# A macaron stack on one core: attention's order of work, routing from logits, and when the last mixture's rows are scattered

## The chip, the core and the metric

The kernel runs on one core of a Trainium2 chip. The metric is the device time of one execution in microseconds (us). The core has TensorE (matrix products and transposes), VectorE, ScalarE and GpSimd (called POOL in the profile), and SyncE (SP), which here issues the plain DMAs; the indirect DMAs, which scatter rows to addresses held in a tile, are issued by POOL. An engine runs its instructions in the order in which the program issued them.

## The reference

Four layers work on x of 4 batches x 512 tokens x 128 channels. Every layer is a macaron: half an FFN, an attention, half an FFN again, each on a layer norm of x.

```python
x = x + 0.5 * ffn(layernorm(x)); x = x + attn(layernorm(x)); x = x + 0.5 * ffn(layernorm(x))
```

- Layer 0: the FFN is a mixture of 8 experts, one choice per token, capacity 320; the attention is causal with 16 heads of 8 and a bias table added to the scores.
- Layer 1: the FFN is a mixture in which every expert is computed for every token; the attention is causal, with no table, and its scores are a product of two factor products.
- Layer 2: the FFN is a two-choice mixture without capacity; in the attention's place stands a gated recurrence.
- Layer 3: the attention is plain (no causal mask); the FFN is a mixture of 8 experts with two choices and capacity 512. Its routing is what most of the diff is about:

```python
scores = softmax(xt @ wg); gates_k, idx_k = top_k(scores, 2)
gates_k = gates_k / sum(gates_k)
m = one_hot(idx_k) as (2*T, E)                 # all first choices, then all second ones
loc = cumsum(m) - 1                            # a token's place in its expert's queue
valid = loc < cap                              # the others are dropped
y = sum_k gates_k * valid * expert_out[idx_k, loc]
```

In layer 0 the choice is the argmax, its weight the largest softmax value, and the place a cumulative sum of the one-hot rows.

## The kernel before

**Mixtures.** `Mixture` holds one expert FFN with scattered tokens: f00 and f01 (layer 0, before and after its attention), f30 and f31 (layer 3). `tokens(bs, ...)` norms the batches `bs` (statistics on VectorE, reciprocal root on POOL by L157/L158, application on VectorE, ScalarE or POOL), transposes, computes the logits on TensorE (L322), chooses (`softmax`, `route`, `without` on VectorE), computes each token's place with two matmuls per choice into `rank` (a triangular matrix of ones on the masks, and a full one on the running sums `pre`), turns it into a row number `to` (L385), copies the weights (L392) and issues one indirect DMA per 128 tokens and choice on POOL (L395, "scatter" below). Places run on from batch to batch through `self.cum`, so the batches' tokens steps follow one another there. `experts` fetches rows from the scattered buffer by SP (`d_f`), transposes them (`dT_f`, L442), and runs two matrix products; it can start only when every scatter of the mixture has landed. `tokens` is a generator: each `yield` ends a step, and the caller decides what is issued between two steps.

**Attention.** `attention` serves layers 0, 1 and 3. A unit is one batch and four heads: 16 units. In the causal layers (the path with `added`, the table or a mask) a unit has four steps, one for each 128 queries, of 128, 256, 384 or 512 keys. The scores of unit u+1 are computed while unit u is worked off: TensorE makes four score banks (L587), VectorE adds the mask and finds the row's extreme in one instruction (L604, L608); POOL subtracts it for two of the four heads (L605), ScalarE takes the exponential of the other two (L617). Four steps later TensorE transposes them (L628), ScalarE takes the exponential of POOL's two (L637) or copies (L639), and TensorE multiplies by the values (L650). In between, each step has two slots for other work: the next batch's `begin` (norm, transposes by `turned`, projections) and, when that is not due, the `after` work of a finished batch: in layer 0 that is f01's `tokens`, with `fine=True`, which cuts it into smaller steps. Layer 1 has layer 3's weights beside it.

All four computing engines' order in `attention` is that of the program text (`manual_schedule`). Between layers 1 and 3 a chain (`behind`) runs FFN, FFN, recurrence, FFN and f30's tokens for batches 0 and 1 together, and 2 and 3 behind them; there POOL's order alone is that of the text and the others' is the scheduler's. In the chain, f30's tokens of the first pair have `later=4`, four empty rounds ahead of the scatters.

**PSUM.** All matmul results share one pool of eight banks (`bank`), given out in rotation.

**Start.** f00's routing runs beside the build of layer 0's bias table: its rows are written to DRAM and read back reversed (`rev`), and TensorE turns them (`turned`, L948).

Of the kernel before, what the change touches and what calls it, by code (L numbers as in the profile page):

```python
# [17 lines left out]
P = 128  # L18
# [23 lines left out]
def kernel(ctx: ExitStack, tc: tile.TileContext, a: dict, out: bass.AP):  # L42
# [25 lines left out]
    for b in range(NB):  # L68
# [13 lines left out]
    before = const([P, P], "before")  # L82
    nc.gpsimd.affine_select(
        out=before, in_=ones, pattern=[[1, P]], compare_op=ALU.is_gt, fill=0.0, base=0, channel_multiplier=-1
    )
    mhalf = const([P, 2 * NT], "mhalf")
# [102 lines left out]
    def turned(n, tag):  # L189

        nT = work.tile([P, S], FP, name=f"nT_{tag}", tag="nT", bufs=4)
        copy(nT, transposed(n, tag))
        yield
        return nT
# [10 lines left out]
    def route(pool, src, g, tag, mask=None):  # L205

        mx = pool.tile([P, g], FP, name=f"mx_{tag}", tag=f"mx_{tag}")
        nc.vector.tensor_reduce(mx, src, AX.X, ALU.max)
# [14 lines left out]

    def softmax(pool, lg, g, tag):

        mx = pool.tile([P, g], FP, name=f"smx_{tag}", tag=f"smx_{tag}")
        nc.vector.tensor_reduce(mx, lg, AX.X, ALU.max)
        pr = pool.tile([P, g, E], FP, name=f"pr_{tag}", tag=f"pr_{tag}")
        nc.vector.tensor_tensor(pr, lg, bc(mx, [P, g, E]), ALU.subtract)
        nc.scalar.activation(pr, pr, AF.Exp)  # L230
        yield
        sm = pool.tile([P, g], FP, name=f"sm_{tag}", tag=f"sm_{tag}")
        nc.vector.tensor_reduce(sm, pr, AX.X, ALU.add)
        nc.vector.reciprocal(sm, sm)
        nc.vector.tensor_tensor(pr, pr, bc(sm, [P, g, E]), ALU.mult)
        return pr
# [4 lines left out]
    class Mixture:  # L241
# [18 lines left out]

        def zeroed(self, pool, tag, bufs=None):

            self.z = pool.tile([P, S], FP, name=f"zeros_{self.tag}", tag=tag, bufs=bufs)
            nc.gpsimd.memset(self.z, 0.0)
# [18 lines left out]
        def tokens(self, bs, wT, on="vector", pool=None, fine=False, later=0):  # L283
# [8 lines left out]
            for n, b in zip(ns, bs):  # L292
# [8 lines left out]

            spare = pool.tile([P, k, G], FP, name=f"spare_{tag}", tag=f"spare{k}{G}")
            nc.gpsimd.tensor_scalar(
                spare, bc_mid(tok_id[:, i0 : i0 + G], [P, k, G]), float(self.rows), None, ALU.add
            )
# [28 lines left out]
            pr = yield from softmax(pool, plg[:, : G * E].rearrange("p (g e) -> p g e", e=E), G, f"r{G}")  # L334
# [15 lines left out]
            if fine:  # L350
                yield
# [1210 lines left out]
```

## Time and profile before

| what | us |
|---|---|
| median of 11 runs | 1558.69 (1554.69 to 1563.63) |
| the profiled execution, its time | 1559.83 |
| its span | 1558.1 |
| TensorE busy in it | 1283.9 (82%) |
| f00: routing; experts | 0 to 60; 61 to 112 |
| layer 0 attention, f01's tokens | 113 to 386 |
| f01: experts; layer 1 FFN | 386 to 540 |
| layer 1 attention | 540 to 790 |
| chain of layers 1 and 2, f30's tokens | 780 to 1047 |
| f30: experts | 1054 to 1121 |
| layer 3 attention, f31's tokens | 1121 to 1465 |
| f31: experts, combine | 1471 to 1558 |

The bounds of the stages are read from the trace and overlap a little. Times are of one profiled execution. A line of a timeline has start, duration, engine, source line, operation, written tile <- read tiles, shape and count, and in brackets how long the engine had stood idle and what released it. A line of waits has who waited, for whom, the sum in us, how often, and the longest. The granted clock is the share of TensorE's full clock that the chip's throttle let through.

### The profile page before, as it was taken

The numbers are of one execution on the slowest core, as the hardware profiler recorded it, in microseconds if no ns is written. First come the engines' busy times: TensorE is split into PE (matmuls) and PEld (weight loads), VectorE is DVE, ScalarE is ACT, GpSimd is POOL, SyncE is SP. The second block draws the span as 40 slices with busy tenths as digits, with TensorE's granted clock in tenths as the row PEclk, the third lists the DMA queues.
The fourth block names the chain that finished last, engine by engine and source line by source line (L and its number), as shares of the span: only waits on it lengthen the run. The fifth ranks groups of instructions, "written<-read, shape, count | busy, mean of one in ns | idle before, by whom it ended". The sixth has DMA issues, their size and how long they took to land. (4 is left out here: it accounts for less than half of the span.)

```text
span 1558.1 us, 28883 instructions
## 1 busy us (share of the span) xinstructions
PE 1283.9 (82%) x10651; PEld 826.0 (53%) x10651; DVE 866.1 (56%) x2955; ACT 712.6 (46%) x1487; POOL 655.7 (42%) x791
## 2 busy tenths in 40 slices
PE   3787998995969688989989887819789999998394
PEld 3464676774755455757656666706533334333273
DVE  5325666773335366666555556615367787773342
ACT  1234876772443156768743322203336655564041
POOL 3455766772420177677610111263631224212253
PEclk9997999996989888999999878858979999999597
DMA  7420230002415375442022000014204000000233
GB/s 227 129 63 7 77 145 31 9 3 62 145 50 110 96 219 147 135 138 69 2 57 54 1 0 1 10 60 103 61 21 171 15 5 12 13 3 15 75 81 103
DMA packets 100660, 106.21 MB, mean 68 GB/s; under 512 B 9084, under 2 KB 73832, under 8 KB 100520
## 3 DMA queue, kind: packets, MB, share of 16 engines
q1 hardware_dynamic: 93864, 91.16, 20.7%
q0 software_dynamic: 6656, 13.22, 2.6%
q8 instruction: 84, 1.38, 0.4%
q14 instruction: 56, 0.46, 0.1%
HBM read 62.49 MB, written 41.85 MB: 67 GB/s over the span
## 5 line engine op out<-in xcount | busy, mean ns | idle before, releaser
L605 POOL TENSOR_SCALAR sc_a<-sc_a,top_a 128x128 f32<-128x128 f32 (+3 forms) x256 | 275.4, 1091 | 115.4 <-DVE top_a L604 77.2
L587 PE MATMUL s_a<-k_a,q_a 32*128 32x512 f32 (+3 forms) x1536 | 266.5, 550 | 17.2 <-DMA k_a<-fac_a 13.8
L692 ACT ACTIVATE w_a<-t_a 128x512 f32<-128x512 f32 x256 | 140.3, 595 | 119.6 <-PE t_a L587 94.8
L628 PE MATMUL t_a<-ident,sc_a 128*128 128x128 f32 x1280 | 173.5, 283 | 5.8 <-DVE top_a L608 5.3
L489 POOL DMA_INDIRECT res_f<-y_f,back_f x112 | 109.6, 979 | 143.6 <-ACT y_f L488 102.7
L587 PE MATMUL t_a<-ql_a,k_a 32*128 32x512 f32 x512 | 168.8, 645 | 0.4 <-DVE low_a__12755 L672 0.2
L628 PEld LDWEIGHTS t_a<-ident,sc_a 128*128 128x128 f32 x1280 | 146.3, 145 | 36.9 <-issue 14.1
L617 ACT ACTIVATE sc_a<-sc_a,top_a 128x128 f32<-128x128 f32 (+3 forms) x256 | 135.0, 577 | 23.2 <-DVE top_a L608 22.9
L587 PEld LDWEIGHTS s_a<-k_a,q_a 32*128 32x128 f32 x1536 | 93.1, 189 | 88.0 <-issue 43.2
L637 ACT ACTIVATE w_a<-t_a 128x256 f32<-128x256 f32 (+2 forms) x192 | 94.3, 526 | 64.4 <-PE t_a L628 64.0
L395 POOL DMA_INDIRECT disp_f<-n_f,to_f x96 | 94.3, 982 | 66.8 <-issue 58.8
L501 PE MATMUL o_f<-w_l,h_f 128*128 128x128 f32 (+1 forms) x896 | 113.0, 279 | 3.8 <-DVE o_f L483 3.3
L501 PEld LDWEIGHTS o_f<-w_l,h_f 128*128 128x128 f32 (+1 forms) x896 | 103.0, 184 | 14.7 <-DVE o_f L483 6.0
L466 PE MATMUL h_f<-dT_f,w_l 128*128 128x320 f32 (+1 forms) x256 | 108.1, 560 | 2.8 <-ACT dT_f L444 2.8
L157 POOL TENSOR_SCALAR rs_f<-mv_f 128x4 f32<-128x4 f32 (+1 forms) x23 | 5.7, 247 | 230.3 <-DVE mv_f L154 229.6
L650 PE MATMUL acc_a<-w_a,vpad 128*32 128x128 f32 x2560 | 98.5, 280 | 0.6 <-DVE top_a L604 0.6
L672 DVE TENSOR_REDUCE low_a__12755<-s_a 128x1 f32<-128x512 f32 x128 | 82.1, 684 | 26.3 <-PE t_a L587 18.5
L639 ACT COPY w_a<-t_a 128x256 f32<-128x256 f32 (+2 forms) x192 | 93.6, 528 | 6.0 <-PE t_a L628 5.8
L608 DVE CUSTOM_DVE_ANT_0 sc_a<-s_a,future 128x128 f32<-128x128 f32 (+3 forms) x128 | 62.3, 486 | 56.4 <-PE s_a L587 43.4
L608 DVE CUSTOM_DVE_ANT_0 sc_a<-s_a,table 128x128 f32<-128x128 f32 (+3 forms) x128 | 62.4, 487 | 54.7 <-PE s_a L587 54.2
L672 DVE TENSOR_REDUCE low_a__12753<-s_a 128x1 f32<-128x512 f32 x128 | 81.2, 682 | 20.1 <-PE t_a L587 15.1
L488 ACT ACTIVATE y_f<-o_f,d_f 128x128 f32<-128x128 f32 (+1 forms) x112 | 38.8, 394 | 105.9 <-DVE o_f L483 105.9
(343 smaller groups left out, 2289.1 us busy)
## 6 DMA issues: line engine op xcount, KB each, us to landing
fac_a<-fac_a_sb SPq DMA_DIRECT2D x36, 256.0 KB
disp_f<-zeros_f SPq DMA_DIRECT2D x4, 2080.0 KB
d_f<-disp_f SPq DMA_DIRECT2D x32, 260.0 KB
w_l<-in_L_ffn_w_dram SPq DMA_DIRECT2D x16, 512.0 KB
cb_f<-rows_f SPq DMA_DIRECT2D x16, 512.0 KB
q_a<-fac_a SPq DMA_DIRECT2D x32, 256.0 KB
k_a<-fac_a SPq DMA_DIRECT2D x32, 256.0 KB
r_f<-res_f SPq DMA_DIRECT2D x24, 256.0 KB
```

The lines of the kernel that those rows point to most:

```text
L395: nc.gpsimd.indirect_dma_start(out=self.to[c][i0 + t][:, :], out_offset=bass.IndirectOffsetOnAxis(ap=to[:, c, t : t + 1], axis=0), in_=ns[ ...
L466: nc.tensor.matmul(ps[u][:, :cap], w1[:, e, (c + u) * P : (c + u + 1) * P], dT, start=True, stop=True)
L489: nc.gpsimd.indirect_dma_start(out=self.back[e * per + s][:, :], out_offset=bass.IndirectOffsetOnAxis(ap=back[:m, s : s + 1], axis=0), in_ ...
L501: nc.tensor.matmul(po[:m, s, :], h[:, c, s * P : s * P + m], w2[:, e, c, :], start=(c == 0), stop=(c == NC - 1),)
L587: nc.tensor.matmul(ps[:, n0:n1], q[r : r + SLOT, i * P : (i + 1) * P], k[r : r + SLOT, n0:n1], start=True, stop=True)
L605: nc.gpsimd.tensor_scalar(sc, sc, top, None, ALU.subtract)
L608: nc.vector.tensor_tensor_reduce(sc, banks[r][:, :n], more, -1.0, HUGE, ALU.add, ALU.min, top)
L617: nc.scalar.activation(sc, sc, AF.Exp, bias=top, scale=-1.0)
L628: nc.tensor.transpose(ps[:, x * n + j * P : x * n + (j + 1) * P], st["sc", u, i, r0 + x][:, j * P : (j + 1) * P], ident,)
L650: nc.tensor.matmul(st["acc", u][r * SLOT : (r + 1) * SLOT, i * P : (i + 1) * P], vpads[b % 2][:, j, g * 4 + r, :], st["w", u, i, r][:, j * ...
L672: nc.vector.tensor_reduce(st["low", u][:, i, c : c + 1], ps, AX.X, ALU.max, negate=True)
L692: nc.scalar.activation(w, ps, AF.Exp)
```

## The change

- **Routing** (all four mixtures): the first choice is taken from the logits, not from softmax values; the exponentials of logits less their maximum serve the second choice and the weights (1 over the sum, or over 1 plus the second's exponential). The masks lie as choice, expert, tile; one scan with a mask of zeros at each expert's first tile (`goes_on`) makes the running sums, and the matmuls take all choices at once, with `not_before` (ones less one) in place of `before`, and a third one for the carried `cum` from the second call on. Spare row numbers and the ends of the experts' queues are made once per mixture on VectorE. Weights are computed behind the rank matmuls, and the row number needs no `keep`.
- **f30's tokens of the first pair:** `later=4` goes; `apart=True` yields after every scatter, and two steps are taken per round of the chain. On POOL the order was: norms of batch 2, norms of batch 3, copies, 16 scatters, 8 and 8. Now: copies and 10 scatters, norms of batch 2, 6 scatters, norms of batch 3, 8 and 8.
- **`turned`:** one more step ahead of the transposes and one behind.
- **Causal attention:** the first of the two slots of a step moves ahead of the next unit's scores, and POOL's subtractions move into `exponentials()`, which is called a step later.

```diff
@@ -79,10 +79,17 @@
-    before = const([P, P], "before")
+    not_before = const([P, P], "not_before")
     nc.gpsimd.affine_select(
-        out=before, in_=ones, pattern=[[1, P]], compare_op=ALU.is_gt, fill=0.0, base=0, channel_multiplier=-1
+        out=not_before, in_=ones, pattern=[[1, P]], compare_op=ALU.is_gt, fill=0.0, base=0, channel_multiplier=-1
     )
+    nc.vector.tensor_scalar(not_before, not_before, -1.0, None, ALU.add)
+    goes_on = {}
+    for g in (NT, 2 * NT):
+        goes_on[g] = const([P, 2 * E * g], f"goes_on{g}")
+        nc.vector.memset(goes_on[g], 1.0)
+        nc.vector.memset(goes_on[g].rearrange("p (e t) -> p e t", t=g)[:, :, 0], 0.0)
...
@@ -188,8 +195,10 @@
     def turned(n, tag):
+        yield
         nT = work.tile([P, S], FP, name=f"nT_{tag}", tag="nT", bufs=4)
         copy(nT, transposed(n, tag))
+        yield
         yield
         return nT
@@ -202,10 +211,11 @@
         return ap.unsqueeze(1).to_broadcast(shape)
-    def route(pool, src, g, tag, mask=None):
-        mx = pool.tile([P, g], FP, name=f"mx_{tag}", tag=f"mx_{tag}")
-        nc.vector.tensor_reduce(mx, src, AX.X, ALU.max)
+    def route(pool, src, g, tag, mask=None, mx=None):
+        if mx is None:
+            mx = pool.tile([P, g], FP, name=f"mx_{tag}", tag=f"mx_{tag}")
+            nc.vector.tensor_reduce(mx, src, AX.X, ALU.max)
         eq = pool.tile([P, g, E], FP, name=f"eq_{tag}", tag=f"eq_{tag}")
...
@@ -220,20 +230,6 @@
         rest = pool.tile([P, g, E], FP, name=f"rest_{tag}", tag=f"rest_{tag}")
         nc.vector.scalar_tensor_tensor(rest, mask, low, src, ALU.mult, ALU.add)
         return rest
-    def softmax(pool, lg, g, tag):
-        mx = pool.tile([P, g], FP, name=f"smx_{tag}", tag=f"smx_{tag}")
-        nc.vector.tensor_reduce(mx, lg, AX.X, ALU.max)
...
-        return pr
     routing = ctx.enter_context(tc.tile_pool(name="routing", bufs=2))
@@ -258,6 +254,15 @@
             self.cum = None
+            self.spare = routing.tile([P, TILES], FP, name=f"spare_{tag}", tag=f"spare{k}", bufs=1)
+            nc.vector.tensor_scalar(self.spare, tok_id[:, :TILES], float(self.rows), None, ALU.add)
+            self.ends = routing.tile([P, k, E, TILES], FP, name=f"ends_{tag}", tag=f"ends{k}", bufs=1)
+            for c, row in enumerate((first_row[self.per], last_row)[:k]):
+                nc.vector.tensor_tensor(
+                    self.ends[:, c], bc(row, [P, E, TILES]), bc_mid(self.spare, [P, E, TILES]), ALU.subtract
+                )
         def zeroed(self, pool, tag, bufs=None):
             self.z = pool.tile([P, S], FP, name=f"zeros_{self.tag}", tag=tag, bufs=bufs)
@@ -280,7 +285,7 @@
-        def tokens(self, bs, wT, on="vector", pool=None, fine=False, later=0):
+        def tokens(self, bs, wT, on="vector", pool=None, fine=False, apart=False):
             pool = pool or routing
             k, G = self.k, len(bs) * NT
@@ -298,11 +303,6 @@
-            spare = pool.tile([P, k, G], FP, name=f"spare_{tag}", tag=f"spare{k}{G}")
-            nc.gpsimd.tensor_scalar(
-                spare, bc_mid(tok_id[:, i0 : i0 + G], [P, k, G]), float(self.rows), None, ALU.add
-            )
             yield from norms([xs[b] for b in bs], rows, tag, on, fine)
             if fine:
                 yield
@@ -331,62 +331,75 @@
                 return pool.tile(shape, dtype, name=f"{name}_{tag}", tag=f"{name}{k}{G}")
             yield
-            pr = yield from softmax(pool, plg[:, : G * E].rearrange("p (g e) -> p g e", e=E), G, f"r{G}")
-            masks = tile("masks", [P, k, G, E])
-            _, best = route(pool, pr, G, f"r0{G}", masks[:, 0])
-            counts = tile("counts", [P, k, G])
-            if k == 1:
-                nc.vector.tensor_scalar(counts[:, 0], best, 0.5, None, ALU.mult)
-            else:
+            lg = plg[:, : G * E].rearrange("p (g e) -> p g e", e=E)
+            mx = tile("mx", [P, G])
+            nc.vector.tensor_reduce(mx, lg, AX.X, ALU.max)
+            pr = tile("pr", [P, G, E])
+            nc.vector.tensor_tensor(pr, lg, bc(mx, [P, G, E]), ALU.subtract)
+            nc.scalar.activation(pr, pr, AF.Exp)
+            masks = tile("masks", [P, k, E, G])
+            by_tile = [masks[:, c].rearrange("p e g -> p g e") for c in range(k)]
+            route(pool, lg, G, f"r0{G}", by_tile[0], mx)
+            yield
+            if k == 2:
+                rest = without(pool, pr, by_tile[0], G, -4.0, f"r{G}")
+                _, second = route(pool, rest, G, f"r1{G}", by_tile[1])
                 if fine:
                     yield
-                rest = without(pool, pr, masks[:, 0], G, -4.0, f"r{G}")
-                _, second = route(pool, rest, G, f"r1{G}", masks[:, 1])
-                total = tile("total", [P, G])
-                nc.vector.tensor_tensor(total, best, second, ALU.add)
-                nc.vector.reciprocal(total, total)
-                nc.vector.scalar_tensor_tensor(counts[:, 0], best, 0.5, total, ALU.mult, ALU.mult)
-                nc.vector.scalar_tensor_tensor(counts[:, 1], second, 0.5, total, ALU.mult, ALU.mult)
-            if fine:
-                yield
-            pre = routing.tile([P, k, G + 1, E], FP, name=f"pre_{tag}", tag=f"pre{k}{G}")
-            if self.cum is None:
-                nc.vector.memset(pre[:, :, 0, :], 0.0)
-            else:
-                nc.vector.tensor_copy(pre[:, :, 0, :], self.cum)
-            for t in range(G):
-                nc.vector.tensor_tensor(pre[:, :, t + 1, :], pre[:, :, t, :], masks[:, :, t, :], ALU.add)
-            self.cum = pre[:, :, G, :]
+            pre = routing.tile([P, k, E, G], FP, name=f"pre_{tag}", tag=f"pre{k}{G}")
+            nc.vector.tensor_tensor_scan(
+                pre.rearrange("p k e g -> p (k e g)"),
+                goes_on[G][:, : k * E * G],
+                masks.rearrange("p k e g -> p (k e g)"),
+                0.0, ALU.mult, ALU.add,
+            )
             yield
             if fine:
                 yield
-            ps = bank(f"rank_{tag}")[:, : k * G * E].rearrange("p (k g e) -> p k g e", k=k, e=E)
-            for c in range(k):
-                out = ps[:, c].rearrange("p g e -> p (g e)")
-                nc.tensor.matmul(out, before, masks[:, c].rearrange("p g e -> p (g e)"), start=True, stop=False)
-                nc.tensor.matmul(out, ones, pre[:, c, :G, :].rearrange("p g e -> p (g e)"), start=False, stop=True)
+            ps = bank(f"rank_{tag}")[:, : k * E * G]
+            nc.tensor.matmul(ps, not_before, masks.rearrange("p k e g -> p (k e g)"), start=True, stop=False)
+            if self.cum is not None:
+                nc.tensor.matmul(
+                    ps.rearrange("p (e g) -> p e g", g=G), ones,
+                    bc(self.cum.rearrange("p k e -> p (k e)"), [P, k * E, G]), start=False, stop=False,
+                )
+            nc.tensor.matmul(ps, ones, pre.rearrange("p k e g -> p (k e g)"), start=False, stop=True)
+            ps = ps.rearrange("p (k e g) -> p k e g", k=k, e=E)
+            counts = tile("counts", [P, k, G])
+            total = tile("total", [P, G])
+            if k == 1:
+                nc.vector.tensor_reduce(total, pr, AX.X, ALU.add)
+            else:
+                nc.vector.tensor_scalar(total, second, 1.0, None, ALU.add)
+            nc.vector.reciprocal(total, total)
+            nc.vector.tensor_scalar(counts[:, 0], total, 0.5, None, ALU.mult)
+            if k == 2:
+                nc.vector.tensor_tensor(counts[:, 1], second, counts[:, 0], ALU.mult)
+            cum = routing.tile([P, k, E], FP, name=f"cum_{tag}", tag=f"cum{k}")
+            if self.cum is None:
+                nc.vector.tensor_copy(cum, pre[:, :, :, G - 1])
+            else:
+                nc.vector.tensor_tensor(cum, self.cum, pre[:, :, :, G - 1], ALU.add)
+            self.cum = cum
             yield
-            kept = tile("kept", [P, k, G, E])
+            kept = tile("kept", [P, k, E, G])
             nc.vector.scalar_tensor_tensor(kept, ps, float(self.cap), masks, ALU.is_lt, ALU.mult)
-            at = tile("at", [P, k, G, E])
-            nc.vector.tensor_tensor(at[:, 0], ps[:, 0], bc_mid(first_row[self.per], [P, G, E]), ALU.add)
+            at = tile("at", [P, k, E, G])
+            nc.vector.tensor_tensor(at[:, 0], ps[:, 0], self.ends[:, 0, :, i0 : i0 + G], ALU.add)
             if k == 2:
-                nc.vector.tensor_tensor(at[:, 1], bc_mid(last_row, [P, G, E]), ps[:, 1], ALU.subtract)
+                nc.vector.tensor_tensor(at[:, 1], self.ends[:, 1, :, i0 : i0 + G], ps[:, 1], ALU.subtract)
             nc.vector.tensor_tensor(at, at, kept, ALU.mult)
             slot = tile("slot", [P, k, G])
-            nc.vector.tensor_reduce(slot, at, AX.X, ALU.add)
-            keep = tile("keep", [P, k, G])
-            nc.vector.tensor_reduce(keep, kept, AX.X, ALU.add)
-            nc.vector.tensor_tensor(slot, slot, spare, ALU.add)
-            nc.vector.tensor_tensor(keep, keep, spare, ALU.mult)
+            nc.vector.tensor_reduce(slot, at.rearrange("p k e g -> p k g e"), AX.X, ALU.add)
             to = tile("to", [P, k, G], I32)
-            nc.vector.tensor_tensor(to, slot, keep, ALU.subtract)
+            nc.vector.tensor_tensor(to, slot, bc_mid(self.spare[:, i0 : i0 + G], [P, k, G]), ALU.add)
             yield
-            for _ in range(later):
-                yield
             for i, n in enumerate(ns):
                 for c in range(k):
                     nc.gpsimd.tensor_copy(n[:, :, 1 if c else D + 3], counts[:, c, i * NT : (i + 1) * NT])
@@ -398,7 +411,7 @@
                         in_=ns[t // NT][:, t % NT, 2 * (1 - c) : 2 * (1 - c) + W],
                         in_offset=None,
                     )
-                    if fine and t % 2:
+                    if apart or (fine and t % 2):
                         yield
             yield
@@ -602,19 +615,23 @@
                 more = added(g * 4 + r)[:, S - n :]
                 if r < 2:
                     nc.vector.tensor_tensor_reduce(sc, banks[r][:, :n], more, 1.0, -HUGE, ALU.add, ALU.max, top)
+                    put_off.append((sc, top, True))
+                else:
+                    nc.vector.tensor_tensor_reduce(sc, banks[r][:, :n], more, -1.0, HUGE, ALU.add, ALU.min, top)
+                    put_off.append((sc, top, False))
+                st["sc", u, i, r] = sc
+        put_off = []
+        def exponentials():
+            for sc, top, less in put_off:
+                if less:
                     nc.gpsimd.tensor_scalar(sc, sc, top, None, ALU.subtract)
                 else:
-                    nc.vector.tensor_tensor_reduce(sc, banks[r][:, :n], more, -1.0, HUGE, ALU.add, ALU.min, top)
-                    put_off.append((sc, top))
-                st["sc", u, i, r] = sc
-        put_off = []
-        def exponentials():
-            for sc, top in put_off:
-                nc.scalar.activation(sc, sc, AF.Exp, bias=top, scale=-1.0)
+                    nc.scalar.activation(sc, sc, AF.Exp, bias=top, scale=-1.0)
             put_off.clear()
         def weights(u, i):
@@ -816,10 +833,10 @@
                         if of:
                             values_up_to(*of)
+                        if rest or not begin_next(u, True):
+                            go_on()
                         if nxt:
                             scores(u + 1, j)
-                        if rest or not begin_next(u, True):
-                            go_on()
                     else:
                         together(step(largest, n + lead), step(by_key, n))
                         if of:
@@ -1494,7 +1511,10 @@
             yield from l2_attn(pool, bs)
             yield from l2_ffn(pool, 1, bs)
             if bs[0] == 0:
-                yield from f30.tokens(bs, l3["gate"], "scalar", pool, later=4)
+                parts = f30.tokens(bs, l3["gate"], "scalar", pool, apart=True)
+                while next(parts, "end") != "end" and next(parts, "end") != "end":
+                    yield
             else:
                 yield from skewed([f30.tokens([b], l3["gate"], "scalar", pool) for b in bs], 3)
```

More of the change, by code (lines that the diff above doesn't have):

```diff
@@ L222, in without @@
         return rest
-    def softmax(pool, lg, g, tag):
-        mx = pool.tile([P, g], FP, name=f"smx_{tag}", tag=f"smx_{tag}")
-        nc.vector.tensor_reduce(mx, lg, AX.X, ALU.max)
-        pr = pool.tile([P, g, E], FP, name=f"pr_{tag}", tag=f"pr_{tag}")
-        nc.vector.tensor_tensor(pr, lg, bc(mx, [P, g, E]), ALU.subtract)
-        nc.scalar.activation(pr, pr, AF.Exp)
-        yield
[L232 to L235, printed above, removed]
-        return pr
     routing = ctx.enter_context(tc.tile_pool(name="routing", bufs=2))
@@ L386, in tokens @@
             yield
-            for _ in range(later):
-                yield
             for i, n in enumerate(ns):
@@ L604, in scores @@
                     nc.vector.tensor_tensor_reduce(sc, banks[r][:, :n], more, 1.0, -HUGE, ALU.add, ALU.max, top)
-                    nc.gpsimd.tensor_scalar(sc, sc, top, None, ALU.subtract)
+                    put_off.append((sc, top, True))
                 else:
                     nc.vector.tensor_tensor_reduce(sc, banks[r][:, :n], more, -1.0, HUGE, ALU.add, ALU.min, top)
-                    put_off.append((sc, top))
+                    put_off.append((sc, top, False))
                 st["sc", u, i, r] = sc
@@ L614, in exponentials @@
         def exponentials():
-            for sc, top in put_off:
-                nc.scalar.activation(sc, sc, AF.Exp, bias=top, scale=-1.0)
+            for sc, top, less in put_off:
+                if less:
+                    nc.gpsimd.tensor_scalar(sc, sc, top, None, ALU.subtract)
+                else:
+                    nc.scalar.activation(sc, sc, AF.Exp, bias=top, scale=-1.0)
             put_off.clear()
```

## The prediction

> **What bounds the kernel now.** I read the page first (the engines' shares), then TensorE's waits over the whole run, then the same waits in the stages that the change touches, and last the timelines of POOL, VectorE and TensorE around the longest of them.
>
> ```profile
> span 1558.1 us, 28883 instructions
> PE 1283.9 (82%) x10651; PEld 826.0 (53%) x10651; DVE 866.1 (56%) x2955; ACT 712.6 (46%) x1487; POOL 655.7 (42%) x791
> ```
>
> TensorE sets the pace, and what is left are its 274 us of idle time. The waits of TensorE, whole run (who waits, for whom, us, times, longest):
>
> ```profile
> PE dT_f L442 <- DMA d_f<-disp_f: 62.6, 4, 34.8
> PE T_a L180 <- DVE n_a L171: 27.5, 10, 10.5
> ```
>
> The first row is the start of each mixture's experts: its rows are scattered by POOL and must all be written before they are fetched. Its 34.8 us are f30's. Of the second row 11.6 us lie in layer 0's attention (125 to 360 us) and 5.4 in layer 1's. POOL's timeline shows what makes f30's scatter late, VectorE's when the rows' numbers were known:
>
> ```profile
> 995.53 0.16 DVE L385 TENSOR_TENSOR to_f<-slot_f,keep_f 128x16 int32<-128x16 f32 x1
> ...
> 1003.04 0.22 POOL L157 TENSOR_SCALAR rs_f<-mv_f 128x4 f32<-128x4 f32 x1 [3.52 <-DVE mv_f L154]
> ...
> 1005.63 1.13 POOL L395 DMA_INDIRECT disp_f<-n_f,to_f  x1 [0.15 <-POOL n_f L392]
> 1007.07 0.96 POOL L395 DMA_INDIRECT disp_f<-n_f,to_f  x1 [0.30 <-issue]
> ```
>
> Pair 0's numbers are there at 995.7, but its 16 scatters stand on POOL behind both norms of batches 2 and 3, whose x comes later: ten us lost. Then 32 scatters follow at 1.262 us each, the last from 1045.77 to 1046.73.
>
> Timelines at the longest gap in layer 0's attention, POOL, then TensorE there and, for the clean pace of 16 transposes, at 161.94:
>
> ```profile
> 129.73 11.28 POOL L605 TENSOR_SCALAR sc_a<-sc_a,top_a 128x128 f32<-128x128 f32 x11
> 140.99 0.22 POOL L157 TENSOR_SCALAR rs_a<-mv_a 128x4 f32<-128x4 f32 x1
> ...
> 142.77 0.59 PE L180 MATMUL T_a<-ident,n_a 128*128 128x128 f32 x2 [2.78 <-DVE n_a L171]
> 145.49 0.69 PE L180 MATMUL T_a<-ident,n_a 128*128 128x128 f32 x2 [2.13 <-DVE n_a L171]
> 145.96 3.62 PE L628 MATMUL t_a<-ident,sc_a 128*128 128x128 f32 x16
> ...
> 161.94 1.91 PE L628 MATMUL t_a<-ident,sc_a 128*128 128x128 f32 x16
> ```
>
> POOL works off subtractions until 140.99 while the next batch's norm waits for its `rstd`; VectorE stands at the norm, TensorE at its transposes. Half of the loss comes behind the gap: the granted clock reads 0.50 from 144 to 150, and 16 transposes take 3.62 us instead of 1.91.
>
> **Part 1, attention's order (layers 0 and 1).** Moved: a step of the next batch's begin (or of f01's tokens) goes ahead of the next unit's scores, POOL's two subtractions per step go into the next step behind that begin, and `turned` gets a slot before and after its transposes. In the program's order, all of batch 1's statistics now precede the scores of unit 1's second step; ten subtractions stand ahead of `rs_a`, not twelve, and VectorE has four score reductions between statistics and norm. Two 256-wide subtractions at 0.92 us (L605's row of that form) less makes `rstd` about 1.8 us earlier; and the transposes stand a whole slot (1.2 us and more of scores or weights) behind the norm.
> - Layer 0: six waits of T_a, 11.6 us (2.78, 2.13, 1.44, 1.07, 3.38, 0.80). I take 9 of them as gone and 2.6 as left. Behind them the clock: 1.71 us on the 16 transposes and 0.4 on the 12 value products after them; at 195.55 1.24 us for eight scores against 0.76 at 169.08, and 2.72 for the four products L901, of which half is 1.36; at 254.98 1.91 us against 1.08 at 193.96, 0.2, 0.5 and 1.2 on what follows: together 6.6 us, of which I take 3. Sum -12. Bounds: -18 if all goes (11.6+6.6), -4 if only the one slot of cover helps (six times 0.7).
> - Layer 1: T_a's waits are 3.66, 0.88 and 0.88, those of `fac_a` for nT 0.68, 1.06 and 1.06: 8.2 in all; the waits for top_a (4.11 at 595.85) sit on a transfer of factors in a stretch where the DMA share is 1.0, and the 2.40 at 701.87 on weights; both stay. But statistics and norms now stand on VectorE ahead of the scores' reductions, so what TensorE no longer waits for in T_a it can wait for in a bank. Taken -2; bounds -10 (8.2, and 2 of clock behind 564, where 0.50 was granted until 570) and +5 (the 4.11 doubled, 1 more).
> - The subtractions come one step (11.5 us a unit, four steps: 2.9 us) later, and are needed four steps after their scores. POOL is 164 of 232 us busy between 125 and 357, and waits 54.4 for top_a: cost nothing while its backlog stays under three steps, 8.6 us.
>
> One rule beside this: the Trainium skill, "TensorE: Matmul & The Clock Gate" (why this matters for your kernels), allows idle gaps up to about 3 us before the clock halves. By the rule, an estimate, only the 3.38 gap would cost clock, the gain above would be 10 us instead of 12 and the time 1534; the rows disagree, since 0.50 was granted behind gaps of 1.44 and 1.07 too, and I go by the rows; 1534 lies inside the forecast.
>
> **Part 2, f30's tokens of pair 0.** Their routing no longer waits four rounds; two steps go per round, a round after each scatter. On VectorE the whole chain of pair 0 now precedes pair 1's `gb_f` (0.68 us each, twelve of them stood inside it), and on TensorE its rank matmuls precede pair 1's gate matmuls. From the logits (VectorE's first row at 978.53): 24 instructions at about 0.22 with the scan, ranks and two hops, 6.5 us: numbers at 985, first scatter 986 instead of 1005.63. POOL's bound is 986 + 32 x 1.262 + norms of batches 2 and 3 (0.22+1.04+0.25+0.20+gaps, 1.9 each) + 1.2 of copies = 1031.5. The price is on pair 1: its x comes about 6 us later (998.76 to 1005), then statistics and POOL's norm 6.2, normalisation and logits 3.8, routing 5.5: batch 3's numbers at about 1020.5, 8 scatters end at 1031. POOL's queue and pair 1 thus end together, and with each waiting for the other at two or three places I take 1036 for 1046.7: -10. Bounds -14 (1032.5) and -4 (pair 1 six us later than taken). The experts' first transposes follow the last scatter by 7.5 us as before (1046.7 to 1054.2).
>
> **Part 3, routing itself.** Of the softmax its sum, reciprocal and product and one of two maxima (two-choice case), the copy and adds of `pre`, keep, its product and the subtraction go; a scan over k x 8 x tiles comes. In the last batch of f31, where nothing else runs, from logits at 1445.58 to numbers at 1453.96: two routes as now end one softmax tail earlier (1448.25 for 1449.4), total, counts and five adds to 1450.9 give way to a scan of 64 elements (estimate 0.3, from 0.69 for a 512-wide product and 1.22 for the scan of 512 in this trace), ranks end at 1449.8 for 1452.24, and three small rows less behind: -2.9 (bounds -1.5, if the scan takes the 512's 1.22, and -4). f01's last batch, one choice, with weight copies still standing between: -1.1 (-2.5 to 0). Layer 3's attention (TensorE 50 of 50 us busy between 1200 and 1400) hides the rest: 0, to -1 or +1.
>
> **Part 4, the start.** The chain to f00's scatters shortens by about 4 us (numbers of the last batch 34.3 for 38.24). But SP's queue now has four loads (reversed table rows, weights) behind the first fetch of scattered rows, and TensorE needs them ahead of dT_f, which started at 59.62, 2.85 after its fetch; such a load lands in 3 to 4.6 us. Taken 0; bounds -3 and +4. New constants add some 1 us to VectorE there, inside these bounds.
>
> **Sum.** -12 -2 -10 -2.9 -1.1 +0 = -28.0. The profiled execution took 1559.83 us (1.7 more than its span), 1.1 above the median of 1558.69; 1559.8-28.0 = 1531.8: I say 1532.
>
> **Rivals.**
> 1. *Stalls only move.* VectorE now has norms ahead of score reductions; nine banks' worth of tiles (one accumulator, four scores, four weights) for eight banks make TensorE wait at t_a or s_a. For it: T_a's waits are really POOL's lateness, and POOL has no less to do. Against it: four reductions now lie between statistics and norm. Part 1 gives 2 instead of 14: 1544.
> 2. *Pair 1 starves the scatter.* Routing and `gb_f` share VectorE; if x of batch 3 comes 7 us later than I take, f30 gains 3, not 10: 1539.
> 3. *Slower: the put-off subtractions are late.* When scatters (1.26 us each, four to eight per batch) and the norms stand ahead of them, the transposes t_a wait for POOL in every step. POOL's 71% speaks for it, its 54.4 us of waiting against. The other parts gain 16 (14 of it in parts 2 and 3, and 2 of part 1 kept); over the 128 steps of two layers it decides at 16/128 = 0.13 us a step. At 0.3 us a step it is 1559.8-16+38 = 1582.
> 4. *No change:* gains of 16 and a loss of 0.13 us a step, 1559.
>
> **Chances.** Forecast (1518 to 1540) 0.57; rival 1 0.17; rival 2 0.09; rival 3 0.12; rival 4 0.05. A difference of 0.2% (3.1 us) is about what a measurement tells from none. Faster 0.57+0.17+0.09 = 0.83, same 0.05, slower 0.12. The range must leave out no more than 0.2: it reaches from the forecast's low end, 1518 (L0 -18, f30 -14, and the tail's -4), to 1550, which holds rivals 1 and 2 and both halves of them together (1551 less one).
>
> **What would show it.** In the changed trace: T_a's waits for n_a in layer 0 under 4 us (11.6 before) and no stretch of 0.50 clock there; otherwise rival 1, which would show in the waits of t_a and s_a. First f30 scatter near 986 on that scale (shifted by what was gained before) and about 50 us to the last one instead of 40; if pauses between scatters sum to over 12 us, rival 2. From f31's last logits to its numbers 5.5 us for 8.4. Rows of TensorE's weight loads waiting for sc_a's subtraction in sum above 10 us (12.6 now, over both layers) would be rival 3. A start of the first dT_f later than 62 us would show that the loads behind the fetch cost more than taken.

## The result and the profile after

The changed kernel takes 1519.24 us (median of 8 runs, 1517.62 to 1521.48) against 1558.04 for the kernel before (31 runs): a ratio of 0.9752, 95% interval 0.9742 to 0.9762. That is 38.8 us less. The forecast was 1532, 28 less, in a range of 1518 to 1550. The profiled execution took 1522.14 us. Its page:

```profile
span 1520.3 us, 28724 instructions
PE 1273.2 (84%) x10645; PEld 819.1 (54%) x10645; DVE 852.0 (56%) x2832; ACT 713.6 (47%) x1487; POOL 653.5 (43%) x776
```

TensorE's record has six matmuls fewer, and it is busy 10.7 us less, so of the 37.8 us of span some 27 are idle time and the rest is almost the same work done in less time. TensorE's waits over the whole run (who waits, for whom, us, times, longest):

```profile
PE dT_f L455 <- DMA d_f<-disp_f: 27.8, 2, 23.3
PE dT_f L455 <- DVE d_f L451: 19.2, 1, 19.2
...
PE T_a L187 <- DVE n_a L178: 12.8, 5, 10.6
...
PE turned L965 <- DMA rev<-tab_rows: 8.5, 1, 8.5
```

The wait for f30's rows is 23.3 us (34.8 before; 5.8 us of it have moved to the waits of T_f and rank ahead of it, 18.2 for 12.4). The second row is f31's wait, 19.1 us long before too. T_a's is down from 27.5 to 12.8, of which 10.6 are the start of layer 0's attention as before, and a wait of 8.5 us for the bias table's rows is new: it took the place of the first wait for scattered rows.

The same stages in both profiles. A length runs from the stage's mark to the next; marks are the first transposes of a mixture's experts (dT_f), the copy that ends a unit of attention (ou_a), and layer 1's first gate transposes (gT). The stretch from f00's dT_f to the last unit of layer 0, "layer 0" below, thus holds f00's experts (61 us) and the attention.

| stage | before | after | change | forecast |
|---|---|---|---|---|
| start to f00's dT_f | 59.6 | 60.2 | +0.6 | 0 |
| to the last unit of layer 0 | 296.6 | 280.5 | -16.1 | -12 |
| to f01's dT_f | 30.2 | 29.1 | -1.1 | -1.1 |
| to gT of layer 1 | 82.1 | 81.6 | -0.5 | 0 |
| to the last unit of layer 1 | 307.9 | 297.3 | -10.6 | -2 |
| chain, to its last projection | 162.2 | 162.3 | +0.1 | 0 |
| to f30's dT_f | 115.4 | 111.2 | -4.2 | -10 |
| to layer 3's first unit | 125.3 | 124.9 | -0.4 | 0 |
| to layer 3's last unit | 251.2 | 248.2 | -3.0 | 0 |
| to f31's dT_f | 41.0 | 38.3 | -2.7 | -2.9 |
| to VectorE's last addition | 83.1 | 82.7 | -0.4 | 0 |

The sum is right to about a quarter, but errors cancel in it: the causal attentions gained 13 us more than forecast and layer 3's attention 3 more, f30 6 less. The lines of f30 after, VectorE and POOL, then TensorE:

```profile
960.03 0.17 DVE L401 TENSOR_TENSOR to_f<-slot_f,spare_f 128x16 int32<-128x16 f32 x1
...
961.02 1.13 POOL L408 DMA_INDIRECT disp_f<-n_f,to_f  x1 [3.00 <-DVE to_f L401]
...
984.16 0.95 POOL L408 DMA_INDIRECT disp_f<-n_f,to_f  x1 [0.30 <-issue]
...
985.66 0.22 POOL L164 TENSOR_SCALAR rs_f<-mv_f 128x4 f32<-128x4 f32 x1
...
994.33 1.12 POOL L408 DMA_INDIRECT disp_f<-n_f,to_f  x1 [6.47 <-DVE masks_f L226]
...
988.19 1.63 PE L187 MATMUL T_f<-ident,n_f 128*128 128x128 f32 x4 [6.54 <-ACT n_f L174]
989.62 0.53 PE L365 MATMUL rank_f<-masks_f,not_before 128*128 128x64 f32 x2
```

Pair 0's scatters do follow its numbers at once (961.02; before, ten us after). But behind the sixteenth of them POOL stands for 6.47 us. Batch 3's norm on POOL (985.66), whose statistics VectorE had ready at 982.0, had waited behind scatters; batch 3's transposes on TensorE (988.19) wait for that norm; and batch 2's rank matmuls, whose masks were ready at 984.4, stand behind those transposes. So two queues cross: early scatters of pair 0 hold up the norm that holds up the ranks that hold up the next scatters.

In layer 0's attention, POOL and TensorE at the place of the forecast's longest gap, in the profile of the same kernel on another chip for POOL's rows (label after_third below):

```profile
127.67 9.69 POOL L632 TENSOR_SCALAR sc_a<-sc_a,top_a 128x128 f32<-128x128 f32 x10 [6.42 <-DVE top_a L617]
137.32 0.24 POOL L164 TENSOR_SCALAR rs_a<-mv_a 128x4 f32<-128x4 f32 x1
```

and in the changed kernel's first profile, TensorE:

```profile
140.39 1.53 PE L645 MATMUL t_a<-ident,sc_a 128*128 128x128 f32 x12
142.18 0.66 PE L645 MATMUL t_a<-ident,sc_a 128*128 128x128 f32 x4 [0.26 <-DVE top_a L621]
...
143.56 0.66 PE L187 MATMUL T_a<-ident,n_a 128*128 128x128 f32 x4
```

Ten subtractions, not twelve, stand ahead of `rs_a`, which comes 10.8 us after the first scores (126.50) and not 13.0 (127.95 in the kernel before). The transposes T_a now stand behind more of the unit's own work and wait for nothing.

### The profile page after: what moved, and what is told of

Its sections match the earlier page's. It is cut to its first block, busy times and chain, and to the rows that moved or that the text cites. A ratio compares the mean times of both kernels' runs of the same rounds, so it can differ in the third digit from the quotient of the medians.

```text
span 1520.3 us, 28724 instructions
## 1 busy us (share of the span) xinstructions
PE 1273.2 (84%) x10645; PEld 819.1 (54%) x10645; DVE 852.0 (56%) x2832; ACT 713.6 (47%) x1487; POOL 653.5 (43%) x776
## 5 line engine op out<-in xcount | busy, mean ns | idle before, releaser
L600 PE MATMUL s_a<-k_a,q_a 32*128 32x512 f32 (+3 forms) x1536 | 260.9, 543 | 19.9 <-POOL k_a L1200 13.7
L502 POOL DMA_INDIRECT res_f<-y_f,back_f x112 | 109.8, 980 | 136.6 <-ACT y_f L501 101.6
L645 PEld LDWEIGHTS t_a<-ident,sc_a 128*128 128x128 f32 x1280 | 142.7, 143 | 41.6 <-issue 16.8
L634 ACT ACTIVATE sc_a<-sc_a,top_a 128x128 f32<-128x128 f32 (+3 forms) x256 | 135.3, 576 | 27.7 <-DVE top_a L621 27.2
L164 POOL TENSOR_SCALAR rs_f<-mv_f 128x4 f32<-128x4 f32 (+1 forms) x23 | 5.7, 250 | 222.5 <-DVE mv_f L161 222.1
L501 ACT ACTIVATE y_f<-o_f,d_f 128x128 f32<-128x128 f32 (+1 forms) x112 | 38.8, 394 | 106.4 <-DVE o_f L496 106.4
L621 DVE CUSTOM_DVE_ANT_0 sc_a<-s_a,table 128x128 f32<-128x128 f32 (+3 forms) x128 | 62.3, 487 | 42.4 <-PE s_a L600 38.4
```

Of the source, the lines that this page charges most:

```text
L502: nc.gpsimd.indirect_dma_start(out=self.back[e * per + s][:, :], out_offset=bass.IndirectOffsetOnAxis(ap=back[:m, s : s + 1], axis=0), in_ ...
L600: nc.tensor.matmul(ps[:, n0:n1], q[r : r + SLOT, i * P : (i + 1) * P], k[r : r + SLOT, n0:n1], start=True, stop=True)
L621: nc.vector.tensor_tensor_reduce(sc, banks[r][:, :n], more, -1.0, HUGE, ALU.add, ALU.min, top)
L634: nc.scalar.activation(sc, sc, AF.Exp, bias=top, scale=-1.0)
L645: nc.tensor.transpose(ps[:, x * n + j * P : x * n + (j + 1) * P], st["sc", u, i, r0 + x][:, j * P : (j + 1) * P], ident,)
```

## The experiments

The groups below ran on three chips, and each chip is slower than that of the first result by its own amount (kernel before: 1574.9, 1570.0 and 1571.0 us). Times are compared as ratios to the kernel before on the same chip, stages mainly between kernels of one group. The edits are shown shortened.

**First group: one part each.** `order_only` is the kernel before with attention's two moves; `turned_only` has the two yields; `routing_only` the routing of all mixtures; `f30_old` is the changed kernel with the old call for pair 0.

```diff
 order_only:   +  if rest or not begin_next(u, True): go_on()   (ahead of scores(u + 1, j))
               +  POOL's subtraction in exponentials()
 turned_only:  +  yield   (ahead of copy(nT, ...))   + yield (behind it)
 f30_old:      -  f30.tokens(..., apart=True), two steps a round
               +  yield from f30.tokens(bs, l3["gate"], "scalar", pool, later=4)
```

> The kernel before with attention's order alone (slot ahead of the scores, POOL's subtractions a step later); turned, routing and f30 as before. Theory A, the order lets rstd come early and puts score reductions between statistics and norm: the waits of T_a in layer 0 fall from 11.6 to about 4 us, TensorE's busy time there falls by some 5 us too as the clock stays up, and the whole is 15 to 20 us faster than before (about 1540). Rival B, the slots in turned are what covers the transposes: the order alone leaves the waits at 8 us or more and gains under 7 (over 1551).

> The kernel before with the two slots in turned alone. Theory A: VectorE still stands at its norm for POOL, so the gap moves from T_a to the score banks and weights; gain 3 to 8 us (about 1552). Rival B: the slots cover the wait, gain 15 us or more (1543 or less).

> The kernel before with the new routing alone (logits, scan, joint rank matmuls), f30 with its four empty rounds, attention and turned as before. Theory A, layer 3's attention got 3.3 us shorter since TensorE bounds it and the rank matmuls fell from 4.7 to 2.9 us there: start +0.6, f01's tail -1.2, layer 3's attention -3, f31's tail -2.7, f30 0 to -2: 1550 to 1552. Rival B, layer 3's gain came from elsewhere (clock, or the earlier stages): layer 3's attention unchanged, 1554 or more.

> The changed kernel with f30's tokens of pair 0 as before (four empty rounds, one step a round, no round after each scatter). Theory A: the 4.2 us gained at f30 are this part's: 1523 to 1524. Rival B: the shorter routing gave them and this part nothing: 1519 to 1520. Rival C: pair 1 was starved by more than the early scatters gave: under 1518.

| kernel | us | ratio (interval) | layer 0 | layer 1 | f30 | layer 3 | f31's tail |
|---|---|---|---|---|---|---|---|
| routing_only | 1560.96 | 0.9907 (0.9889 to 0.9926) | 296.6 | 308.7 | 115.7 | 255.6 | 38.4 |
| order_only | 1561.93 | 0.9927 (0.9902 to 0.9951) | 294.8 | 301.9 | 117.6 | 256.4 | 39.9 |
| turned_only | 1554.56 | 0.9880 (0.9862 to 0.9898) | 287.4 | 301.7 | 117.7 | 256.3 | 40.3 |
| f30_old | 1537.39 | 0.9762 (0.9738 to 0.9786) | 280.9 | 298.2 | 115.7 | 255.2 | 38.1 |

Columns are the stages of the first table in us. In the attentions `routing_only` stands for the kernel before.
- Layer 0: the order alone gives 1.8 us, the slots in `turned` 9.2, both 15.7. But this stretch begins with f00's experts, and these took 59 us in `routing_only` and `f30_old` against 61 and 62 in the other two, at a granted clock of 0.93 against 0.89, though no edit touches them. In the attention alone (237.8 us, 233.9, 225.7 and 222.1 in `f30_old`) the order gives 3.9 us, the slots 12.1 and both 15.7: the parts add up, and the slots are the larger one.
- By the ratios, on the scale of the first result, `order_only` gains 11 us, between theory A's 15 to 20 and rival B's "under 7": neither holds, though T_a's waits fell as A has it. `turned_only` gains 19, as its rival B has it. TensorE's waits between 125 and 358 us show what is left with the order alone:

```profile
PE t_a L632 <- DVE top_a L608: 5.9, 7, 1.8
PE T_a L180 <- DVE n_a L171: 3.2, 4, 1.6
```

T_a's wait went from 12.1 (in `routing_only`) to 3.2, but 5.9 us came up at t_a: part of the stall moved, as the forecast's first rival says. That T_a still follows its norm directly there is the likely reason; it was not tested apart. With `turned` alone T_a has left the list of waits of 0.2 us and more; 2.5 us came up at t_a and 4.4 at f01's own transposes.
- Layer 1: 6.8, 7.0 and 10.5 us. Here each does most of it alone.
- f30: the routing gives 2 us there (115.7 for 117.6), the hurried call nothing in sum: 115.7 with the old call, and 115.6 and 115.5 in two profiles of the changed kernel below, on other chips. In time 0.9762 against 0.9752 to 0.9788. Of `f30_old`'s theories B holds, though in the first pair of profiles the stage gained 4.2. Counted from layer 1's last unit, the last scatter ends at 268.7 us with the old call and at 270.5 in `after_again`, and the fetch behind it is issued 4.0 and 1.9 us later; why that last wait differs was not looked into.
- Layer 3: the new routing is worth 0.8 us (255.6 for 256.4), not 3; the tail of f31 1.5 to 1.9 here. `routing_only` gains 14 us by its ratio, where theory A said 6 to 8 and its rival less: neither holds.
- What stays open: of these 14 us the stages place about 6 beside `order_only`'s (f01's tail, f30, layer 3, f31's tail), and f00's experts 2 more. The profiled execution of `routing_only` is also 1.8 us above its median and that of `order_only` 3.1 below, so such a difference of stages comes out up to 5 us too small. No profile of the kernel before was taken on that chip. By the medians there the three parts gain 13.9, 13.0 and 20.3 us, 47 in sum; all of them together (`f30_old`) 37.5.

**Second group: the same kernels again, a later round, the table's loads.**

```diff
 lag4:   - yield from skewed([f30.tokens([b], ...) for b in bs], 3)
         + yield from skewed([f30.tokens([b], ...) for b in bs], 4)
 start:  - whole(skewed(choices, 2)); whole(made)
         + whole(skewed(choices + [made], 2))
```

> The kernel before, unchanged, for its profile on the chip of this group: the stages as on record, their lengths within some us, to compare the next three stage by stage.

> The changed kernel, unchanged, on the chip of this group: a ratio near 0.975. If half of the gain in the causal attentions is the clock, TensorE's busy time between the first and the last unit falls by as much as its idle time, in layer 0 some 8 us each. If layer 3's attention gains by its rank matmuls it is about 2 us shorter; if its 3.3 us were the chip's, it is within 1 us.

> The changed kernel with batch 3's tokens of f30 one round later behind batch 2's (4 for 3). POOL's order is the same; on TensorE the rank matmuls of batch 2 now stand ahead of batch 3's transposes. Theory A, the crossing starves the scatter (six scatters ahead of batch 3's norm on POOL, that norm ahead of batch 2's ranks on TensorE): POOL's 6.5 us pause ahead of batch 2's scatters goes, the last scatter comes 4 to 6 us earlier, the whole 1514. Rival B, batch 2's numbers are late by VectorE or by x itself: pause and time unchanged, 1519.

> The changed kernel with the second half of layer 0's bias table issued between the batches of f00's routing and not behind them, so its last loads stand ahead of the first fetch of scattered rows in SP's queue. Theory A, the 8.5 us wait for rev is the queue's order: the first dT_f at about 56 for 60.2, the whole 1515. Rival B, the weight loads that move ahead with them wait for their buffers and hold the fetch: dT_f at 60 or later, no gain.

| kernel | us | ratio (interval) | start | layer 0 | layer 1 | f30 | layer 3 |
|---|---|---|---|---|---|---|---|
| before_again | 1569.57 | one run | 59.6 | 297.6 | 305.2 | 117.9 | 258.3 |
| after_again | 1537.19 | 0.9788 (0.9758 to 0.9818) | 59.0 | 281.1 | 297.9 | 115.6 | 255.2 |
| lag4 | 1528.18 | 0.9725 (0.9690 to 0.9760) | 60.2 | 280.7 | 298.1 | 109.7 | 255.1 |
| start | 1544.84 | 0.9833 (0.9803 to 0.9863) | 68.1 | 282.8 | 295.8 | 115.1 | 255.5 |

Layer 0's gain, -16.5 us on this chip, split by busy time. The kernel before, f00's experts and then the attention (stretch, its length, busy us and counts of the engines, TensorE first, then granted clock, DMA share, GB/s):

```profile
59.60:120.90 61.30, 49.37 (x281) 36.85 (x281) 19.27 (x60) 19.90 (x48) 27.62 (x30) 0.89 0.23 62
120.90:357.20 236.30, 219.63 (x2640) 155.95 (x2640) 158.93 (x708) 167.68 (x363) 165.38 (x169) 0.96 0.14 48
```

and the changed kernel:

```profile
59.00:117.80 58.80, 46.84 (x282) 35.53 (x282) 19.51 (x61) 20.29 (x50) 28.23 (x32) 0.93 0.21 58
117.80:340.00 222.20, 212.88 (x2644) 150.26 (x2644) 154.53 (x684) 168.04 (x363) 164.97 (x165) 0.99 0.16 51
```

2.5 us of the gain lie in f00's experts, where TensorE is busy that much less at a higher granted clock. In the attention TensorE does almost the same work (2640 and 2644 matmuls in the record): of 14.1 us, 6.7 are busy time and 7.3 idle time (16.7 to 9.3). On the first pair it is 15.7 us (235.6 to 219.9), 7.7 of them busy and 8.0 idle, and the experts differ by 0.4. So the expectation, that busy time falls by as much as idle time, some 8 us each, is about met: half of the attention's gain is TensorE's busy time, and the granted clock there rises from 0.96 to 0.99 (first pair 0.94 to 0.99). Layer 3's attention is 3.1 us shorter on this chip (first pair 3.0). Over the groups it takes 255.1 to 255.6 us with the new routing (253.3 in `lag4_revq` below) against 256.3 to 258.3 without: 1 to 3 us. The rows of the rank matmuls in that stage sum to 4.7 us before and 2.9 after in the first pair, but they overlap: TensorE is busy with one for 3.2 us and 2.1. These 1.1 us account for the smaller gains; the rest of the 3 us is not placed.

`lag4` changes nothing on POOL and puts batch 2's rank matmuls ahead of batch 3's transposes on TensorE. Its rows, POOL and TensorE:

```profile
989.36 0.20 POOL L169 TENSOR_TENSOR off_f<-off_f,rstd_f 128x4 f32<-128x4 f32 x1
989.50 0.32 POOL L405 COPY n_f<-counts_f 128x4 f32<-128x4 f32 x2
990.14 1.12 POOL L408 DMA_INDIRECT disp_f<-n_f,to_f  x1 [0.32 <-POOL n_f L405]
...
986.19 0.66 PE L365 MATMUL rank_f<-masks_f,not_before 128*128 128x64 f32 x2 [2.92 <-DVE counts_f L383]
...
990.14 1.63 PE L187 MATMUL T_f<-ident,n_f 128*128 128x128 f32 x4 [2.44 <-ACT n_f L174]
```

POOL's pause is 0.32 us for 6.47, f30's stage 5.9 us shorter, the time 9.0 us (medians, with intervals that overlap). Theory A, the crossing, holds; the stage is the sure number.

`start` shows the other side. The last rows of the table and weights now stand ahead of the first fetch in SP's queue:

```profile
50.63 0.25 SPq L1362 DMA_DIRECT2D gb_rows<-in_L_attn_ln_beta_dram  x1
54.84 0.36 SPq L144 DMA_DIRECT2D raw_sg1T<-in_L_ffn_ws_gate_dram  x1
55.44 0.36 SPq L144 DMA_DIRECT2D raw_su1T<-in_L_ffn_ws_up_dram  x1
65.28 1.44 SPq L439 DMA_DIRECT2D d_f<-disp_f  x3
```

The experts start at 68.1, 9 us later than in `after_again`. Theory A falls and rival B's time comes, but not by its cause: the queue is free at 55.8, and the fetch is issued only at 65.28, behind the last scatter (62.7 for 47.8 in `after_again`). On TensorE the table's matmuls now stand ahead of the third batch's logits and wait there for their rows, so that batch's numbers come at 52.7 us for 37.5.

**Third group: the two halves of attention's order, and a better start.** `slot_old` and `subs_at_once` each undo one half in the changed kernel; `lag4_revq` is `lag4` with the table's rows loaded from ScalarE's queue.

```diff
 slot_old:      the first slot of a step behind scores(u + 1, j) again
 subs_at_once:  -  put_off.append((sc, top, True))
                +  nc.gpsimd.tensor_scalar(sc, sc, top, None, ALU.subtract)
 lag4_revq:     -  nc.sync.dma_start(rev, ...)
                +  nc.scalar.dma_start(rev, ...)
```

> The changed kernel with the first slot of a step behind the next unit's scores again, the subtractions still put off. Theory A, the place of the slot relieves the norm: the two causal attentions lose most of what the order gave beside turned, 5 to 9 us (1525 to 1528 on the scale of the changed kernel's 1519). Theory B, it is POOL's subtractions: within 2 us of the changed kernel.

> The changed kernel with POOL's subtractions issued at once, the slot still ahead of the scores. Theory A, the slot: within 2 us of the changed kernel, since the begin's norm precedes the step's own subtractions anyway. Theory B, the put-off: 5 to 9 us slower, VectorE waits for rstd again. If the put-off is a loss (the subtractions come late), 1 us or more faster.

> The changed kernel with batch 3's tokens a round later, and the reversed table rows loaded from ScalarE's queue, not SP's. Theory A, the 8.5 us wait at the start is the order in SP's queue: first dT_f at 54 to 56 for 60, the whole 4 to 6 us under the run with the later round alone. Rival B, the loads of weights ahead of the fetch wait for the same buffers: 59 or later, no gain.

> The changed kernel, unchanged, for its profile on the chip of this group: stages as in its other profiles but for what chips differ in.

| kernel | us | ratio (interval) | start | layer 0 | layer 1 | f30 |
|---|---|---|---|---|---|---|
| after_third | 1537.27 | one run | 60.2 | 281.9 | 298.3 | 115.5 |
| slot_old | 1543.76 | 0.9824 (0.9799 to 0.9849) | 59.5 | 287.7 | 298.5 | 115.2 |
| subs_at_once | 1552.51 | 0.9883 (0.9857 to 0.9910) | 60.2 | 288.7 | 305.0 | 115.5 |
| lag4_revq | 1524.01 | 0.9706 (0.9678 to 0.9734) | 54.0 | 283.4 | 297.8 | 109.8 |

Neither theory on the two halves is enough. Without the slot's move layer 0 loses 5.8 us, without the put-off 6.8 (6.0 and 6.5 in the attention alone). Either loss is more than the two halves bring beside `turned` in the first group (225.7 to 222.1), so there they work only together; layer 1 loses nothing without the first (0.2) and 6.7 without the second. In time they are 6.5 and 15.2 us over the changed kernel's one run. With the slot in its old place and the subtractions still put off, TensorE's waits from 113 to 350 us have a row that no other kernel here shows at this size:

```profile
PE t_a L645 <- POOL sc_a L632: 5.5, 4, 2.8
```

That is the forecast's third rival in small: put-off subtractions that come late, here behind scatters that wait for their numbers (POOL stands 5.8 us ahead of a scatter at 336.95; the longest of the waits, 2.8 us, ends at 341.02). The slot's move is what keeps it away (0.2 us in the changed kernel, in layer 1). In `subs_at_once`, layer 1:

```profile
PE t_a L641 <- DVE top_a L621: 5.5, 5, 4.2
PE s_a L600 <- DVE top_a L621: 4.1, 1, 4.1
```

against 3.0 and 3.1 in the changed kernel on that chip. The wait of 4.2 is the stall that the forecast put down to a transfer of factors and left standing; it shrinks to 1.7 when the subtractions are put off. In both kernels VectorE waits there for the factors (q_a from fac_a, 4.6 and 2.0 us), so the forecast had the cause right; with the put-off the next batch's `rs_a` comes earlier, and the transfer with it.

`lag4_revq` starts its experts at 54.0 for 60.2, as theory A has it, the table's eight loads being out of SP's queue, and keeps 5.7 us at f30. In time it is 0.9706 for `lag4`'s 0.9725 on another chip, 3 us where 4 to 6 were expected, with intervals that overlap. Its dT_f row on TensorE:

```profile
53.98 0.61 PE L455 MATMUL dT_f<-ident,d_f 128*128 128x128 f32 x3 [2.75 <-DMA d_f<-disp_f]
```

At 0.9706 of the kernel before it is the fastest of all: 13 us under the changed kernel's one run on the same chip, of which f30 is 5.7 and the start 4.7 (6.2, less 1.5 that the next stage gives back, in f00's experts: TensorE is busy 48.5 us there for 47.0, at a granted clock of 0.91 for 0.93); the other 3 lie in layer 3's stages and were not looked into.

## Why the prediction was right, and where it was off

- **Sum.** 1519.2 lies inside the range near its low end, and the sign and most of the mechanism were right. The likeliest time was 13 us too long. That it lies inside is partly luck: had f30 gained its 10 us and not 4.2, the time would have been some 1513, below the range.
- **Layer 0, -12 for -16.1 (-16.5 on the second chip).** The mechanism is shown: T_a's waits fell from 11.6 us to 0.5 where 4 were allowed, and the granted clock reads 1.00 from 127 to 344 us, where the kernel before had 0.50 in four stretches of 3 to 7 us. The slots in `turned` are worth about three times the order (12.1 and 3.9 us, first group). The mis-sized term is the clock: "together 6.6 us, of which I take 3". In the attention TensorE's busy time fell by 7.7 (6.7 on the second chip), so the 6.6 of the list were about right and the halving was the error. The idle term, 9 taken, came to 8.0 (7.3); t_a's waits for VectorE took back 2.8 (2.9).
- **The clock's rule.** The sentence of the Trainium skill on gaps of about 3 us ("TensorE: Matmul & The Clock Gate", why this matters for your kernels) would have made the gain smaller, 10 for 12. The runs went the other way: behind the pair of gaps of 2.78 and 2.13 us the clock read 0.50 in all three profiles that have T_a's waits unchanged (`before`, `before_again`, `routing_only`), and the busy time came back with the pair gone. Behind the pair of 1.44 and 1.07 us it read 0.50 in two of them and 1.00 in `before_again`, and in `before` it read 0.50 from 225.6 us behind a single gap of 0.82 us, which cost nothing in `before_again`. So the lengths of the gaps do not settle it alone here; what else does was not tested.
- **Layer 1, -2 for -10.6 (-7.3).** The step "what TensorE no longer waits for in T_a it can wait for in a bank" was mis-sized. It happened once: 2.9 us of the first gap are now a wait of s_a for VectorE. But T_a, `fac_a` and t_a together fell from 13.5 us (5.4, 2.8, 5.3) to 3.9 (1.8, 0, 2.1), the stall that was to stay (4.11 at 595.85) among them. And TensorE's busy time between the first and the last unit fell by 4.4 (186.1 us to 181.7, granted clock 0.96 to 0.99), a term that the likely value put at nothing. The bound on that side, -10, was just passed on the first pair of profiles.
- **f30, -10 for -4.2 (-2.3).** "POOL's queue and pair 1 thus end together" failed. Pair 0's numbers came within three us of the time forecast and the scatters began at once, but the forecast looked at POOL's queue and at pair 1's data apart and did not look for what stands behind batch 3's transposes on TensorE. `lag4` shows that crossing to be worth 5.9 us. Rival 2 (pair 1 starves the scatter, f30 gains 3) gives the size, but the cause is a queue more than x: less the 27.7 us that the chain ahead had gained, batch 3's x comes 8.5 us late (979.52 for 998.76) where 6 were taken, and its logits 10.5 (990.8 for 1008.0). Between the two lies the norm on POOL, which starts 3.7 us after its statistics are ready.
- **Tails, -2.9 and -1.1 for -2.7 and -1.1; start, 0 for +0.6.** Right. At the start the new loads behind the fetch took what the shorter routing gave: the first fetch is issued 6.2 us earlier (50.58 for 56.77), but rev's wait of 8.5 us is new, and `lag4_revq` gains 6.2 by taking these loads off the queue. One reading was wrong: the numbers at 38.24 are the second batch's; the last batch's came at 45.5 and now come at 43.1.
- **Layer 3, 0 for -3.** I set the routing's edits there at nothing "because TensorE is busy 50 of 50 us"; that hides VectorE's share, but the rank matmuls are TensorE's own work, 1.1 us of its busy time. The rest of the 3 us is not placed.
- **Rivals 1 and 3** did not happen in the changed kernel. (The sign named for rival 3, weight loads that wait for POOL's subtraction above 10 us, could not tell much, as it stood at 12.6 before; it is 9.7 after.) Both appear when a part is missing: rival 1 with the order alone (t_a 5.9 us), rival 3 with the slot in its old place (5.5 us).

## What to carry to other kernels

When a stall is removed, count the busy time behind it too: in these profiles TensorE mostly ran at half its clock for 3 to 7 us behind pairs of short gaps, and in layer 0's attention that was worth as much as the gaps. When work is hurried on one queue, list for each other queue what stands behind the first instruction that this delays; a crossing of two queues (scatter ahead of a norm, transposes ahead of ranks) takes back the gain and shows as a pause of an engine whose data is ready elsewhere. On the engine that sets the pace, no edit is hidden: its own instructions count. And look whether a stage that is compared holds work that no edit touches: f00's experts moved by 2 to 3 us between profiles and hid in layer 0's numbers.

## What was not expected of the hardware

The profile of layer 3's attention, where TensorE is idle for 0.4 to 4 us, took 251.2 and 248.2 us on the first pair and 253 to 258 on three other chips, and the whole kernel before 1558 to 1575 us: between chips a stage can differ by more than an edit moves it, so stages were mainly compared within a chip. f00's experts, the same matmuls in every kernel, took TensorE 46.8 to 49.7 us of busy time, at a granted clock of 0.93 to 0.89. A plain DMA from ScalarE's queue, 8 of them in the middle of its activations, cost nothing that the stages show, unless it is the 1.5 us in f00's experts; but `start`, whose loads are on SP, is just as slow there (48.6 us of TensorE's busy time for 48.5), so that is not shown.
